# Graph attention on one core: edge projection and Q's selection produced with edges on partitions

## The chip, the cores and the metric

The kernel runs on one core of a Trainium2 chip. The metric is device time in microseconds (us) of one execution, lower is better. Engines: PE is TensorE, DVE is VectorE, ACT is ScalarE, POOL is GpSimd, SP is SyncE, which issues most plain transfers. "A gather" below is one indirect DMA that GpSimd issues: it fetches one row per partition for 128 edges.

## The reference, cut to what matters

One graph-attention layer with 8 heads of 16 columns over 12,500 nodes and 212,500 edges sorted by destination, then a residual, a batch norm over the nodes, a second residual and a layer norm.

```python
Q, K, V = x @ WQ, x @ WK, x @ WV              # 12500 x 128, as 8 heads of 16
Eh = edge_attr_128 @ WE                       # 212500 x 128
score = K[src] * Q[dst] / sqrt(16) * Eh       # per edge, 128 columns
score = exp(clip(score.sum(-1), -5, 5))       # per edge and head
wV = segment_sum(V[src] * score, dst);  Z = segment_sum(score, dst)
h = x + wV / (Z + 1e-6)
h = batchnorm(h) * gamma + beta
out = layernorm(x + h)
```

## The kernel before

**Layout.** Edges are cut into 1661 tiles of 128. A group `g` has two halves of four tiles (`halves(g)`; `G = 8`, `U = 4`), there are 208 groups, and the last one has 3 + 2 tiles. The destinations of one half lie in a window of 64 nodes.

**Set-up.** A table of K and V (`kvd`, one row of 256 floats per node) is computed from x and written to DRAM (`table_rows`, L634). Meanwhile GpSimd gathers rows of x for the first 64 tiles, eight groups; these are turned (`turn_x`, L261) and projected (`project`, L268), three groups during set-up and the other five ("late" groups) inside the loop.

**Gathers.** Every later tile needs one gather of K and V, 128 rows of 1 KB (L202), issued in order on GpSimd's own queue. `load_kv` queues the eight gathers of a group as soon as a slot is free; after the start there are nine slots, so the gathers of group g + 9 wait for `message(g)`.

**The loop** (L759 to L822) is written out by hand: each engine runs its instructions in the order of these calls, and nothing reorders them. Iteration g works on several groups at once. What each step does, with its line:

- `eh_mm` (L510), for g + 2: the edge projection, as two matmuls with `WE` stationary and the transposed edge features moving, so that the result has columns on partitions and 512 edges along the row. `eh_out` (L517): ScalarE copies it to SBUF (`wt`).
- `q_mm`, `q_out` (L483, L487), for g + 4: Q of the group's two windows, to SBUF as float32. `q_hi`, `q_rest`, `q_mid`, `q_lo` (L491 to L501), for g + 3 and g + 2: Q is split into three bfloat16 parts, two steps on ScalarE and two subtractions on VectorE.
- `turned_onehot` (L473), for g + 3: a bfloat16 one-hot matrix (node against edge). `qe_mm` (L525), for g + 2: six matmuls, three parts by two halves, select Q for each edge.
- `both` (L535), for g + 1: VectorE multiplies the two in columns-on-partitions form. `turn_back` (L543), for g + 1: eight transposes on TensorE bring the product to edges on partitions.
- `products` (L558), for g: VectorE multiplies the gathered K in place by it, one instruction for each half. This is the first step that needs the gather.
- `scores` (L565), `clip_exp` (L574 to L576), `message` (L580), for g: the score by head, its exponential, and V times it.
- `onehot` (L463 to L466) and `gather_sum` (L595, L596): the sum over edges into nodes on TensorE, for g - 1.
- `denom`, `recip`, `attn` (L605, L608, L612), for g - 2, and `add_x`, `x_out` (L621, L622, L626), for g - 3: the quotient and the residual.

**PSUM.** Eight banks: two named `ps_e`, two `ps_q`, two `ps_t`, one `ps_a` and one `ps_m`.

**The end** (L823 to L889, then `last_stage`): the last two groups half by half, the norm's sums, and the layer norm over all nodes.

Of the kernel before, what the change touches and what calls it, by code (L numbers as in the profile page):

```python
# [8 lines left out]
F32 = mybir.dt.float32  # L9
BF16 = mybir.dt.bfloat16  # L10
# [7 lines left out]
P = 128  # L18
# [42 lines left out]
def gnn_kernel(  # L61
# [199 lines left out]
    def turn_x(g, a, act=None):  # L261
        XT[g, a] = wp.tile([P, 4, P], F32, name="xt", bufs=2)
        ps = turned()
# [4 lines left out]
    def project(g, a, ps_kv, act=None):  # L268
        for c in (0, 2):
            ps = ps_kv()  # L270
# [151 lines left out]
    EA, OH, OT, Q3, XW, BASE, MSG, QE, OS, AT, AGG, WT, PW = ({} for _ in range(13))  # L422
# [13 lines left out]
    def project_main(g):  # L436
        half = [table_tile(2 * (g % 2) + a) for a in (0, 1)]
        KV[g] = lambda a, b, c, n=P: half[a // 4][:, a % 4:a % 4 + b - a, c:c + n]
        for a in (0, 4):
            project(g, a, lambda: turned().rearrange("p (a b) d -> p a (b d)", b=2), True)  # L440
# [28 lines left out]
    def turned_onehot(g):  # L469

        OT[g] = wp.tile([P, U * P], BF16, name="ot", bufs=2)
        if usizes[2 * g] == usizes[2 * g + 1] == U:
            nc.vector.tensor_scalar(OT[g], RB[g], wiota, None, op0=OP.is_equal)  # L473
# [5 lines left out]
    PQ, QS, QR = {}, {}, {}  # L479
# [9 lines left out]
    def q_hi(g):  # L489
        Q3[g] = wp.tile([P, 3, P], BF16, name="q3", bufs=2)  # L490
        nc.scalar.activation(Q3[g][:, 0, :], QS[g], AF.Copy)  # L491

    def q_rest(g):
        QR[g] = QS[g]
        nc.vector.tensor_sub(QR[g], QS[g], Q3[g][:, 0, :])

    def q_mid(g):
        nc.scalar.activation(Q3[g][:, 1, :], QR[g], AF.Copy)

    def q_lo(g):  # L500
        nc.vector.tensor_sub(Q3[g][:, 2, :], QR[g], Q3[g][:, 1, :])  # L501

    EH = {}

    def eh_mm(g):

        EH[g] = []
        for a, b in halves(g):
            eh = psp.tile([P, U * P], F32, name="ps_e", bufs=2)[:, :(b - a) * P]
            nc.tensor.matmul(eh, w_e, EA[g][:, a:b, :].rearrange("p a b -> p (a b)"), start=True, stop=True)  # L510
            EH[g].append(eh)

    def eh_out(g):
        WT[g] = []
        for h, (a, b) in enumerate(halves(g)):
            t = wp.tile([P, U * P], F32, name="wt", bufs=4)
            nc.scalar.activation(t[:, :(b - a) * P], EH[g][h], AF.Copy)  # L517
            WT[g].append(t)

    def qe_mm(g):  # L520
        QE[g] = [psp.tile([P, U * P], F32, name="ps_q", bufs=2)[:, :(b - a) * P] for a, b in halves(g)]
        for k in range(3):
            for h, (a, b) in enumerate(halves(g)):
                r = slice(h * WN, (h + 1) * WN)
                nc.tensor.matmul(QE[g][h], Q3[g][r, k, :], OT[g][r, :(b - a) * P], start=(k == 0), stop=(k == 2))  # L525

    def ehqe(g):
        eh_mm(g)
        eh_out(g)
        qe_mm(g)  # L530

    def both(g, h):
        a, b = halves(g)[h]
        t = WT[g][h][:, :(b - a) * P]
        nc.vector.tensor_tensor(t, t, QE[g][h], op=OP.mult)  # L535

    def turn_back(g):

        PW[g] = []
        for h, (a, b) in enumerate(halves(g)):  # L540
            ps = turned()
            for j in range(b - a):
                nc.tensor.transpose(ps[:, j, :], WT[g][h][:, j * P:(j + 1) * P], ident)  # L543
            PW[g].append(ps)
# [9 lines left out]
    def products(g, hs=(0, 1)):  # L554
        for i in hs:
            a, b = halves(g)[i]
            kv = KV[g](a, b, 0)
            step = nc.vector.tensor_tensor(kv, kv, PW[g][i][:, :b - a, :], op=OP.mult)  # L558
            PARTS.setdefault(g, []).append(step)
# [58 lines left out]
    def add_x(g):  # L618
        NEW[g] = ps = (psp.tile([P, 4, P], F32, name="ps_t", bufs=2)[:, 0, :] if NG - 3 <= g < NG - 1 else
                       small_ps[:, 1, :] if g >= NG - 4 else sum_ps[:, W + P:W + 2 * P])  # L620
# [40 lines left out]
    def both_halves(g):  # L661
        both(g, 0)
        both(g, 1)


    steps = [[(locate,)], [(place, runs[0])], [], [(q_mm, 0), (q_out, 0), (q_hi, 0)],
             [(q_rest, 0), (q_mid, 0), (load_rel, 0)], [(q_lo, 0), (load, 0)],
             [(q_mm, 1), (q_out, 1), (q_hi, 1), (load_rel, 1)],
             [(q_rest, 1), (q_mid, 1)], [(q_lo, 1), (load_rel, 2)], [(load, 1)], [(turned_onehot, 0)],
# [4 lines left out]
    for q in range(NQ):  # L674
# [11 lines left out]
        for g, a in piece.get(q, []):  # L686
            project(g, a, wide)
# [9 lines left out]
    ehqe(0)  # L697
    q_mm(2)
    q_out(2)
    q_hi(2)  # L700
    both_halves(0)
    q_rest(2)
    q_mid(2)
    turn_back(0)
    ehqe(1)
    within(load, 2)
    turned_onehot(2)
    load_rel(3)
    q_window(3)
    q_window(4)  # L710
    q_mm(3)
    q_out(3)
    load_rel(4)
    load(3)
# [17 lines left out]
    RING = ["ps_e", "ps_e", "ps_q", "ps_q", "ps_t", "ps_t", "ps_a", "ps_m"]  # L732
# [26 lines left out]
    for g in range(NG - 2):  # L759
        within(load, g + 4)  # L760
        within(load_rel, g + 5)
        if (g + 6) % RQ == 0 and (g + 6) // RQ in quads:
            load_quad((g + 6) // RQ)
        within(q_hi, g + 3)
        within(products, g)
        within(q_lo, g + 2)
# [4 lines left out]
        within(turned_onehot, g + 3)  # L771
        within(both_halves, g + 1)
# [29 lines left out]
        within(q_mid, g + 3)  # L802
# [29 lines left out]
    both_halves(last)  # L832
    attn(g - 2)
    add_x(g - 3)
    issue()
    gather_sum(g - 1)
# [3 lines left out]
    turn_back(last)  # L840
# [309 lines left out]
```

## Time and profile before

| | |
|---|---|
| median of 3 runs | 2141.98 us (2141.85 to 2142.24) |
| the profiled execution, its own time | 2143.53 us |
| its span, first to last instruction | 2141.1 us |
| mean granted TensorE clock | 0.917 |
| PE busy | 1710.7 us (80%) |
| DVE busy | 1590.1 us (74%) |
| ACT busy | 670.6 us (31%) |
| POOL busy | 1606.6 us (75%) |
| mean DMA rate | 180 GB/s |

Busy time is the union of an engine's instructions. A row of a group of instructions reads: line, engine, operation, output <- inputs, shape, count | busy us, mean ns of one | idle time of the engine just before them, and what ended most of it. "<-issue" means that no wait that the profile knows ended just then. A row of a timeline reads: start us, duration us, engine, line, operation, and in brackets the idle time before it.

### The profile page before, as it was taken

The page shows a single profiled execution, that of the slowest core. Times are in us where ns is not written, and L with a number is a line of the kernel's source. Part 1 is how long each engine was busy: PE and PEld are TensorE (multiplying, and loading weights), DVE is VectorE, ACT ScalarE, POOL GpSimd, SP SyncE. Part 2 cuts the span into 40 slices and gives each one's busy share as a digit, 9 for nine tenths or more (in the row PEclk, how much of TensorE's full clock was granted, in tenths as well). Part 3 has the DMA queues.
Part 4 walks back from the last instruction along what each step waited for, and adds up shares of the span by engine and source line. Part 5 has one row for each costly group of instructions (what it writes and reads, how often), then busy time and mean ns, then how long its engine had stood idle before and what let it go on. Part 6 is the DMA issues. An engine that isn't in the chain of part 4 may idle for free. (4 is left out here: it accounts for less than half of the span.)

```text
span 2141.1 us, 31269 instructions
## 1 busy us (share of the span) xinstructions
PE 1710.7 (80%) x9414; PEld 1100.9 (51%) x9414; DVE 1590.1 (74%) x3555; ACT 670.6 (31%) x2688; POOL 1606.6 (75%) x1697
## 2 busy tenths in 40 slices
PE   8899998777868778877778778777878877778777
PEld 7576565444545445544445445545545545544456
DVE  4679998777777777777677777677777777777786
ACT  3454343223223223222223223223223222223225
POOL 7777777777777777777777777777777777777775
PEclk9999999998998998899898998898898898898899
DMA  9957666565565565565565565565565565565574
GB/s 306 308 177 201 188 198 183 165 182 166 165 183 158 171 183 163 167 183 165 165 183 158 172 183 163 167 184 160 169 184 159 170 184 161 167 184 164 170 235 125
DMA packets 172648, 386.41 MB, mean 180 GB/s; under 512 B 35950, under 2 KB 88727, under 8 KB 172471
## 3 DMA queue, kind: packets, MB, share of 16 engines
q0 software_dynamic: 78704, 213.62, 34.6%
q1 hardware_dynamic: 90404, 169.36, 25.9%
q8 instruction: 78, 1.28, 0.3%
q10 hardware_dynamic: 3363, 1.34, 0.2%
q14 instruction: 99, 0.81, 0.1%
HBM read 364.56 MB, written 19.63 MB: 179 GB/s over the span
## 5 line engine op out<-in xcount | busy, mean ns | idle before, releaser
L202 POOL DMA_INDIRECT slot<-kvd,srcs x1597 | 1517.8, 950 | 486.4 <-issue 409.4
L558 DVE TENSOR_TENSOR slot<-slot,ps_t 128x512 f32<-128x512 f32 x410 | 276.7, 682 | 453.2 <-DMA slot<-kvd,srcs 412.3
L543 PE MATMUL ps_t<-ident,wt 128*128 128x128 f32 x1661 | 283.9, 313 | 385.9 <-DVE wt L535 384.1
L596 PE MATMUL ps_a<-msg,oh 128*128 128x136 f32 (+1 forms) x3322 | 524.4, 297 | 2.1 <-DVE msg L580 2.1
L543 PEld LDWEIGHTS ps_t<-ident,wt 128*128 128x128 f32 x1661 | 211.7, 159 | 562.3 <-issue 501.2
L596 PEld LDWEIGHTS ps_a<-msg,oh 128*128 128x128 f32 (+1 forms) x3322 | 425.2, 171 | 81.5 <-issue 53.8
L575 ACT ACTIVATE ps_m<-s 128x64 f32<-128x64 f32 (+1 forms) x209 | 47.5, 227 | 1125.4 <-DVE s L574 1060.9
L510 PE MATMUL ps_e<-ea,w_e 128*128 128x512 f32 x832 | 390.6, 591 | 0.7 <-ACT wt L517 0.7
L535 DVE TENSOR_TENSOR wt<-wt,ps_q 128x512 f32<-128x512 f32 x416 | 264.4, 675 | 2.6 <-PE ps_q L525 2.6
L580 DVE TENSOR_TENSOR msg<-slot,ps_m 128x1024 f32<-128x1024 f32 (+2 forms) x209 | 248.0, 1188 | 0.4 <-ACT ps_m L575 0.3
L565 DVE TENSOR_REDUCE s<-slot 128x64 f32<-128x1024 f32 (+1 forms) x208 | 248.1, 1194 | 0.1
L517 ACT ACTIVATE wt<-ps_e 128x512 f32<-128x512 f32 x416 | 233.8, 620 | 13.3 <-PE ps_e L510 13.2
L525 PE MATMUL ps_q<-ot,q 64*128 64x512 bf16 x1248 | 213.3, 457 | 0.0
L510 PEld LDWEIGHTS ps_e<-ea,w_e 128*128 128x128 f32 x832 | 143.0, 190 | 100.7 <-issue 98.5
L463 DVE TENSOR_TENSOR oh<-ps_m,rel_i 128x512 f32<-128x512 f32 x208 | 141.4, 680 | 0.0
L491 ACT ACTIVATE q<-qs 128x128 bf16<-128x128 f32 x208 | 64.3, 309 | 217.3 <-PE ps_q L525 186.6
L621 PEld LDWEIGHTS ps_a<-ident,at 128*128 128x128 f32 x408 | 71.7, 221 | 111.7 <-issue 56.0
L621 PE MATMUL ps_a<-ident,at 128*128 128x128 f32 x408 | 115.4, 370 | 2.5 <-DVE relrow L322 2.3
L626 ACT ACTIVATE hx<-ps_a 128x64 f32 x408 | 87.9, 215 | 33.9 <-PE ps_a L596 27.2
L452 ACT ACTIVATE xw<-hx 128x64 f32 x416 | 88.2, 280 | 11.1 <-DMA hx<-xT 6.5
L525 PEld LDWEIGHTS <-q 64*128 64x128 bf16 x1248 | 48.9, 103 | 80.9 <-issue 64.4
L622 PE MATMUL ps_a<-xw,ident 128*128 128x128 f32 x408 | 89.7, 306 | 0.0
(175 smaller groups left out, 1618.9 us busy)
## 6 DMA issues: line engine op xcount, KB each, us to landing
ea<-eaT SPq DMA_DIRECT2D x207, 512.0 KB, 3.8
slot<-kvd,srcs POOLq DMA_INDIRECT x1597
rbq<-relT SPq DMA_DIRECT2D x94, 256.0 KB, 6.6
kvd<-slot SPq DMA_DIRECT2D x12, 512.0 KB, 7.1
kvd<-t SPq DMA_DIRECT2D x12, 512.0 KB, 6.8
slot<-xT SPq DMA_DIRECT2D x24, 256.0 KB, 5.2
out<-o SPq DMA_DIRECT2D x23, 256.0 KB, 3.2
hx<-xT SPq DMA_DIRECT2D x11, 512.0 KB, 7.7
```

The lines of the kernel that those rows point to most:

```text
L202: return nc.gpsimd.indirect_dma_start(out=out, out_offset=None, in_=table, in_offset=bass.IndirectOffsetOnAxis(ap=srcs[:, e:e + 1], axis=0))
L463: nc.vector.tensor_tensor(one, iota_ps[:, None, :].to_broadcast([P, n, P]), r[:, :n, None].to_broadcast([P, n, P]), op=OP.is_equal)
L510: nc.tensor.matmul(eh, w_e, EA[g][:, a:b, :].rearrange("p a b -> p (a b)"), start=True, stop=True)
L517: nc.scalar.activation(t[:, :(b - a) * P], EH[g][h], AF.Copy)
L525: nc.tensor.matmul(QE[g][h], Q3[g][r, k, :], OT[g][r, :(b - a) * P], start=(k == 0), stop=(k == 2))
L535: nc.vector.tensor_tensor(t, t, QE[g][h], op=OP.mult)
L543: nc.tensor.transpose(ps[:, j, :], WT[g][h][:, j * P:(j + 1) * P], ident)
L558: step = nc.vector.tensor_tensor(kv, kv, PW[g][i][:, :b - a, :], op=OP.mult)
L565: step = nc.vector.tensor_reduce(SS[g][:, a:b, :], KV[g](a, b, 0).rearrange("p t (h d) -> p t h d", d=DH), axis=AX.X, op=OP.add)
L580: step = nc.vector.tensor_tensor(MSG[g][:, a:b, :P].rearrange("p t (h d) -> p t h d", d=DH), KV[g](a, b, P).rearrange("p t (h d) -> p t h ...
L596: nc.tensor.matmul(AGG[g][WN if j >= n else 0:], OH[g][j], MSG[g][:, j, :], start=(j == 0), stop=(j == n - 1))
L621: nc.tensor.matmul(ps, AT[g], ident, start=True, stop=False)
```

## The change

- The edge projection has the edge features stationary and `WE` moving, one matmul for each tile, so that its result lies in PSUM with edges on partitions.
- Q's selection is one float32 matmul for each tile: the one-hot matrix (now float32) stationary, the half's float32 Q moving. The three-part split is gone.
- `products` multiplies the gathered K twice, by the one and by the other, both read from PSUM. `eh_out`, `both` and `turn_back` are gone.
- One ring of six PSUM banks (`ps`) takes the place of `ps_e`, `ps_q` and `ps_t`. A group's four results fill four of the six, so its first half is computed before `gather_sum` and its second half after it, for g + 1 in iteration g.
- The steps ahead run at smaller distances: `load` g + 3, `load_rel` g + 4, `turned_onehot` g + 2, `q_mm` and `q_out` g + 2, `q_window` g + 3.
- `add_x` of the last four groups writes to `ps_m`.

```diff
+    def bank():
+        return psp.tile([P, 4, P], F32, name="ps", bufs=6)
+
     def wide():
-        t = psp.tile([P, 4, P], F32, name=("ps_e", "ps_q")[turn[0] % 2], bufs=2)
-        return t.rearrange("p (a b) d -> p a (b d)", b=2)
-
-    def turned():
-        return psp.tile([P, 4, P], F32, name="ps_t", bufs=2)
+        return bank().rearrange("p (a b) d -> p a (b d)", b=2)
...
     def turned_onehot(g):
-        OT[g] = wp.tile([P, U * P], BF16, name="ot", bufs=2)
+        OT[g] = wp.tile([P, U * P], F32, name="ot", bufs=2)
...
-    def q_hi(g):
-    def q_rest(g):
-    def q_mid(g):
-    def q_lo(g):
-    def eh_mm(g):
-    def eh_out(g):
-    def qe_mm(g):
-    def both(g, h):
-    def turn_back(g):
+    def eh_qe(g, hs=(0, 1)):
+        for h in hs:
+            a, b = halves(g)[h]
+            r = slice(h * WN, (h + 1) * WN)
+            EH[g, h], QE[g, h] = bank(), bank()
+            for j in range(a, b):
+                nc.tensor.matmul(EH[g, h][:, j - a, :], EA[g][:, j, :], w_e, start=True, stop=True)
             for j in range(b - a):
+                nc.tensor.matmul(QE[g, h][:, j, :], OT[g][r, j * P:(j + 1) * P], QS[g][r], start=True, stop=True)
...
             kv = KV[g](a, b, 0)
-            step = nc.vector.tensor_tensor(kv, kv, PW[g][i][:, :b - a, :], op=OP.mult)
+            nc.vector.tensor_tensor(kv, kv, EH[g, i][:, :b - a, :], op=OP.mult)
+            step = nc.vector.tensor_tensor(kv, kv, QE[g, i][:, :b - a, :], op=OP.mult)
...
     for g in range(NG - 2):
-        within(load, g + 4)
-        within(load_rel, g + 5)
+        within(load, g + 3)
+        within(load_rel, g + 4)
-        within(q_hi, g + 3)
         within(products, g)
-        within(q_lo, g + 2)
         within(denom, g - 2)
         within(scores, g)
         within(clip_exp, g)
         within(recip, g - 2)
-        within(turned_onehot, g + 3)
-        within(both_halves, g + 1)
+        within(turned_onehot, g + 2)
...
         within(add_x, g - 3)
-        within(q_mm, g + 4)
+        within(q_mm, g + 2)
...
+        if not late_x:
+            eh_qe(g + 1, (0,))
         within(gather_sum, g - 1)
-        if not late_x:
-            within(eh_mm, g + 2)
         within(x_out, g - 3)
-        within(q_out, g + 4)
+        within(q_out, g + 2)
         within(sums_out, g - 1)
         if late_x:
             project_main(g + 1)
-            within(eh_mm, g + 2)
-        within(eh_out, g + 2)
-        within(q_window, g + 5)
-        within(turn_back, g + 1)
-        within(qe_mm, g + 2)
+            eh_qe(g + 1, (0,))
+        eh_qe(g + 1, (1,))
+        within(q_window, g + 3)
         within(attn, g - 2)
-        within(q_rest, g + 3)
-        within(q_mid, g + 3)
         within(message, g)
         within(onehot, g + 1)
...
     products(g, (0,))
-    both_halves(last)
     attn(g - 2)
     add_x(g - 3)
     issue()
+    eh_qe(last, (0,))
     gather_sum(g - 1)
     x_out(g - 3)
     sums_out(g - 1)
     products(g, (1,))
-    turn_back(last)
+    eh_qe(last, (1,))
```

More of the change, by code (lines that the diff above doesn't have):

```diff
@@ L420, in load_x @@
                 nc.sync.dma_start(XR[i][:, :width(i)], xT[:, i * B4:i * B4 + width(i)])
-    EA, OH, OT, Q3, XW, BASE, MSG, QE, OS, AT, AGG, WT, PW = ({} for _ in range(13))
+    EA, OH, OT, XW, BASE, MSG, QE, OS, AT, AGG = ({} for _ in range(10))
     def nt(g):
@@ L487, in q_out @@
         nc.scalar.activation(QS[g], PQ[g], AF.Copy, scale=0.25)
-    def q_hi(g):
-        Q3[g] = wp.tile([P, 3, P], BF16, name="q3", bufs=2)
-        nc.scalar.activation(Q3[g][:, 0, :], QS[g], AF.Copy)
-    def q_rest(g):
-        QR[g] = QS[g]
-        nc.vector.tensor_sub(QR[g], QS[g], Q3[g][:, 0, :])
-    def q_mid(g):
-        nc.scalar.activation(Q3[g][:, 1, :], QR[g], AF.Copy)
-    def q_lo(g):
-        nc.vector.tensor_sub(Q3[g][:, 2, :], QR[g], Q3[g][:, 1, :])
-    EH = {}
-    def eh_mm(g):
[L507 to L511, printed above, removed]
-    def eh_out(g):
[L514 to L518, printed above, removed]
-    def qe_mm(g):
[L521 to L530, printed above, removed]
-    def both(g, h):
-        a, b = halves(g)[h]
-        t = WT[g][h][:, :(b - a) * P]
-        nc.vector.tensor_tensor(t, t, QE[g][h], op=OP.mult)
-    def turn_back(g):
-        PW[g] = []
-        for h, (a, b) in enumerate(halves(g)):
-            ps = turned()
+    EH = {}
+    def eh_qe(g, hs=(0, 1)):
[5 more added lines that the diff above has]
+                nc.tensor.matmul(EH[g, h][:, j - a, :], EA[g][:, j, :], w_e, start=True, stop=True)
             for j in range(b - a):
-                nc.tensor.transpose(ps[:, j, :], WT[g][h][:, j * P:(j + 1) * P], ident)
-            PW[g].append(ps)
+                nc.tensor.matmul(QE[g, h][:, j, :], OT[g][r, j * P:(j + 1) * P], QS[g][r], start=True, stop=True)
     SENT, PARTS = {}, {}
@@ L618, in add_x @@
     def add_x(g):
-        NEW[g] = ps = (psp.tile([P, 4, P], F32, name="ps_t", bufs=2)[:, 0, :] if NG - 3 <= g < NG - 1 else
-                       small_ps[:, 1, :] if g >= NG - 4 else sum_ps[:, W + P:W + 2 * P])
+        NEW[g] = ps = small_ps[:, g % 2, :] if g >= NG - 4 else sum_ps[:, W + P:W + 2 * P]
         nc.tensor.matmul(ps, AT[g], ident, start=True, stop=False)
@@ L660, in gnn_kernel @@
         piece.setdefault(3 + k * (NQ - 4) // (2 * early), []).append((k // 2, 4 * (k % 2)))
[L661 to L669, printed above, removed]
+    steps = [[(locate,)], [(place, runs[0])], [], [(q_mm, 0), (q_out, 0)],
+             [(load_rel, 0)], [(load, 0)],
+             [(q_mm, 1), (q_out, 1), (load_rel, 1)],
+             [], [(load_rel, 2)], [(load, 1)], [(turned_onehot, 0)],
              [(turned_onehot, 1)]]
@@ L696, in gnn_kernel @@
     load_kv()
[L697 to L705, printed above, removed]
+    eh_qe(0)
     within(load, 2)
-    turned_onehot(2)
     load_rel(3)
[L709 to L714, printed above, removed]
     onehot(0)
@@ L731, in gnn_kernel @@
     AHEAD = [0, 1, 2, 3, 4, 5, 6, 12, 18]
-    RING = ["ps_e", "ps_e", "ps_q", "ps_q", "ps_t", "ps_t", "ps_a", "ps_m"]
+    RING = ["ps"] * 6 + ["ps_a", "ps_m"]
     def blocks(i):
```

12 lines of the change are left out of this document (6 added, 6 removed).

## The prediction

> **What bounds the kernel now.** I began with the busy times and then asked for GpSimd's own rows, because a busy share of three quarters hides what fills the rest.
>
> ```profile
> PE 1710.7 (80%) x9414; PEld 1100.9 (51%) x9414; DVE 1590.1 (74%) x3555; ACT 670.6 (31%) x2688; POOL 1606.6 (75%) x1697
> ```
>
> No engine looks full. The costliest group of instructions and the view of its line (shortest, median and longest duration) say more:
>
> ```profile
> L202 POOL DMA_INDIRECT slot<-kvd,srcs x1597 | 1517.8, 950 | 486.4 <-issue 409.4
> ```
>
> ```profile
> L202 POOL DMA_INDIRECT slot<-kvd,srcs x1597: 942/946/1197, 83.4 to 2086.4; - x200
> ```
>
> A gather takes 0.946 us, and 486.4 / 1597 = 0.304 us lies ahead of each: a pitch of 1.25 us. GpSimd's timeline, first and last of 1661 gathers:
>
> ```profile
> 3.04 1.15 POOL L202 DMA_INDIRECT slot<-x,srcs  x1 [1.87 <-DMA srcs<-src]
> ...
> 2086.38 0.95 POOL L202 DMA_INDIRECT slot<-kvd,srcs  x1 [0.30 <-issue]
> ```
>
> From 3.04 to 2087.33 are 2084.3 us, and 1661 x 1.25 = 2076. So there is no wait longer than the 0.30 us gap anywhere: the gathers are one unbroken line, and 53.8 us follow it. The execution's own 2143.53 us are 3.0 of start + 2084.3 + 53.8 + 2.4 outside the span. The time can change in only three ways: gathers wait, a gather itself takes another time, or the last 53.8 us change. Eight gathers, 10.0 us, are the budget of a group.
>
> The gathers do not all take 0.946. The mean is 0.950, so 1517.8 - 1597 x 0.946 = 7.0 us are excess. I set the start of each gather against what VectorE was running. In 54 cases a gather of over 0.995 us begins while `attn` (L612) or `q_rest` (L495) runs, 5.3 us in all; the first and the last:
>
> ```profile
> 99.63 0.28 DVE L495 TENSOR_TENSOR qs<-qs,q 128x128 f32<-128x128 f32 x1
> 99.65 1.08 POOL L202 DMA_INDIRECT slot<-kvd,srcs  x1 [0.30 <-issue]
> ...
> 2031.24 0.28 DVE L495 TENSOR_TENSOR qs<-qs,q 128x128 f32<-128x128 f32 x1
> ...
> 2031.30 1.03 POOL L202 DMA_INDIRECT slot<-kvd,srcs  x1 [0.30 <-DVE wt L535]
> ```
>
> The first gather is 0.13 too long and L495 ends 0.26 after its start; the second 0.087, and 0.22. Both fit one rule: a gather needs something 0.13 us after its start that the VectorE instruction holds until its own end, if that instruction started at least 0.02 us sooner. The holders read two SBUF tensors, or are the one-hot (L473). Products with PSUM (L558, L535) hold nobody up.
>
> [...]
>
> **Where VectorE stands against the gathers.** One period of VectorE from the moment T at which the last gathered rows of a group land, and GpSimd in the same stretch:
>
> ```profile
> 1009.69 0.69 DVE L558 TENSOR_TENSOR slot<-slot,ps_t 128x512 f32<-128x512 f32 x1 [1.92 <-DMA slot<-kvd,srcs]
> 1010.29 0.28 DVE L501 TENSOR_TENSOR q<-qs,q 128x128 bf16<-128x128 f32 x1
> 1010.49 0.17 DVE L605 TENSOR_SCALAR rz<-os 128x8 f32<-128x8 f32 x1
> 1010.57 1.21 DVE L565 TENSOR_REDUCE s<-slot 128x64 f32<-128x1024 f32 x1
> 1011.81 0.23 DVE L574 TENSOR_SCALAR s<-s 128x64 f32<-128x64 f32 x1
> 1011.96 0.19 DVE L608 RECIPROCAL rz<-rz 128x8 f32<-128x8 f32 x1
> 1012.08 0.30 DVE L473 TENSOR_SCALAR ot<-rbq,wiota 128x512 bf16<-128x512 bf16 x1
> 1012.29 1.27 DVE L535 TENSOR_TENSOR wt<-wt,ps_q 128x512 f32<-128x512 f32 x2
> 1013.49 0.34 DVE L612 SCALAR_TENSOR_TENSOR at<-os,keep,rz 128x128 f32<-128x128 f32 x1
> 1013.75 0.28 DVE L495 TENSOR_TENSOR qs<-qs,q 128x128 f32<-128x128 f32 x1
> 1013.95 1.21 DVE L580 TENSOR_TENSOR msg<-slot,ps_m 128x1024 f32<-128x1024 f32 x1
> ```
>
> ```profile
> 1006.82 0.95 POOL L202 DMA_INDIRECT slot<-kvd,srcs  x1 [0.30 <-issue]
> ...
> 1013.07 0.95 POOL L202 DMA_INDIRECT slot<-kvd,srcs  x1 [0.30 <-DVE wt L535]
> ```
>
> T = 1009.69 is 2.87 us after the start of the group's last gather, 1006.82, so VectorE's steps stand at a fixed phase to the gathers: five pitches later a gather starts at T + 3.38. Now the one-hot runs at T + 2.39 to 2.69 and `attn` with `q_rest` at T + 3.80 to 4.34, so that gather starts in the free stretch between. In 88 of the 165 groups from 40 to 204 this distance is 2.82 to 2.94 us; in the others other transfers make it longer, at any phase.
>
> **The change part by part.**
>
> *TensorE.* Busy times of what goes, and the loads of fourteen float32 pairs (weight load and matmul) in a dense stretch:
>
> ```profile
> L510 PE MATMUL ps_e<-ea,w_e 128*128 128x512 f32 x828 | 389.3, 592 | 0.7 <-ACT wt L517 0.7
> ...
> L543 PE MATMUL ps_t<-ident,wt 128*128 128x128 f32 x1661 | 283.9, 313 | 385.9 <-DVE wt L535 384.1 <-DVE slot L558 1.0
> ...
> L525 PE MATMUL ps_q<-ot,q 64*128 64x512 bf16 x1242 | 212.6, 458 | 0.0
> ```
>
> ```profile
> 1015.68 1.78 PEld L596 LDWEIGHTS ps_a<-msg,oh 128*128 128x128 f32 x14
> ```
>
> (389.3 + 283.9 + 212.6) / 208 = 4.26 us of a group go. A float32 matmul is two pairs here (L543, a transpose, is one for each tile, L510 two for each half), so 8 tiles x 2 matmuls x 2 = 32 pairs come, at 1.78 / 14 = 0.127: 4.07 us. TensorE stays at 1710.7 / 208 - 0.2 = 8.0 us of the 10.0. The order adds a wait: the second half of g + 1 takes the banks of the first half of g, so it stands behind that product, and `add_x`, `q_mm` and the next first half are queued behind it. VectorE makes that product when four gathers have landed, about 5 us ahead of T, so the wait has ended long before T. Cost nothing, under cover of the 2 us that TensorE has over.
>
> *ScalarE.* Three copies of the group go. It is 31% busy; nothing on the line of gathers waits for it. Nothing.
>
> *VectorE, total.* `q_rest` and `q_lo` go (0.28 each). `both` becomes the second multiply of `products`: the same count, shape and operand kinds. The one-hot writes float32. The nearest row of a float32 VectorE comparison:
>
> ```profile
> L311 DVE TENSOR_SCALAR lim<-lim 128x416 f32<-128x416 f32 x1 | 0.4, 421 | 0.0
> ```
>
> For 512 elements that is between 0.42 and 0.42 x 512 / 416 = 0.52; against it stand 0.30 (L473, if only the input's type counts) and 0.69 (L558's full rate). I take 0.47, nearest to L311. In all 1590.1 / 208 = 7.6 us become 7.6 - 0.56 + 0.17 = 7.2 of 10.0: still under the budget, so nothing directly.
>
> [...]
>
> *VectorE, phase.* This is what I take to count. After T two multiplies depend on each other. A dependent neighbour starts 0.04 us after the end:
>
> ```profile
> 2090.70 0.42 DVE L558 TENSOR_TENSOR slot<-slot,ps_t 128x256 f32<-128x256 f32 x1 [1.22 <-DMA slot<-kvd,srcs]
> 2091.16 0.42 DVE L565 TENSOR_REDUCE s<-slot 128x16 f32<-128x256 f32 x1
> ```
>
> So the second starts at T + 0.72, `scores` at T + 1.44 (now 0.88), and the one-hot, 1.50 later as now, at T + 2.94 to 3.41. `attn` follows directly, since `both` no longer stands between: like L535 after L473 it starts 0.09 before the end, so T + 3.32 to 3.66. The gather that starts at T + 3.38 needs the port at 3.51 and gets it at 3.66: 0.15 us late. It happens where the gather starts 0.02 or more after `attn`, a distance of at most 2.91 us: 66 of 165 groups, 83 of 208, so 83 x 0.15 = 12.5 us. [...] The 5.3 us at `attn` and `q_rest` go, since `q_rest` is the instruction that holds in nearly all of them. The groups at other phases pay for 0.72 us of one-hot and `attn` where they pay for 0.92 of three instructions now; I count that as even. Net +7.
>
> Bounds: with VectorE 0.15 us earlier or later by a little more, `attn` misses all of them: 0 - 5.3 = -5. If the one-hot catches them instead, 111 x 0.25 (twice L473's hold) = 28, net +22.
>
> *The last 53.8 us.* The last product (2090.70) waited for its rows, and VectorE had 1.22 us to spare. The second multiplies of group 206's second half (0.72) and of group 207's first (0.57) take those, and the last one adds 0.42 + 0.04: +0.5.
>
> *The start.* `eh_mm` ran two groups ahead, now one. The five late groups are TensorE's:
>
> ```profile
> 105.60:160.00 54.40, 54.40 (x334) 39.53 (x333) 39.07 (x96) 30.09 (x89) 41.06 (x44) 1.00 0.58 176
> ```
>
> Its busy time fills the stretch, 11 us a group. The tightest point after it is the slot of group 8, given free by `message(8)` and refilled by group 17:
>
> ```profile
> 162.03 1.21 DVE L580 TENSOR_TENSOR msg<-slot,ps_m 128x1024 f32<-128x1024 f32 x1
> ```
>
> ```profile
> 173.92 0.94 POOL L202 DMA_INDIRECT slot<-kvd,srcs  x1 [0.30 <-issue]
> ```
>
> 10.7 us to spare. With TensorE's work equal, nothing; the cover ends at 10.7 / 5 = 2.1 us more for each late group. The SP loads keep their distance from use (`load` and its reader both moved by one), so no queue is newly blocked.
>
> **The sum.** 2143.53 + 7 + 0.5 = 2151.0 for a profiled execution. The median of the runs lies 1.55 below the profiled one now, so the forecast is 2149.
>
> **The rivals.** About 0.2% (4.3 us) is what a measurement of this kernel can tell from no change.
>
> *Clear of the port* (18%). `q_rest`'s holds go and `attn` falls between gathers. It decides within 0.1 us of phase, and the multiply's true delay or a one-hot of 0.30 would do it. 2142 - 5.3 + 0.5 = 2137.
>
> *The one-hot catches the gathers* (15%). It needs 0.1 to 0.2 us more delay than I reckon. Net +13 to +22, so 2155 to 2165.
>
> *TensorE becomes the bound* (3%). If a pair cost 0.30, the mean of one matmul, and not 0.127, a group would take 8.2 - 4.26 + 32 x 0.30 = 13.5 us: some 700 us slower. It decides from 0.19 a pair. Dense rows speak against it.
>
> *The start stalls* (4%). With 4 us more for each late group, 20 - 10.7 = 9 us: 2158.
>
> *The change does little because all of it is hidden*, the two phase terms cancelling: this is the lower part of my forecast case, +0.5 to +4.
>
> **The numbers.** My case (60%) reaches from 2142.5 to 2155, a third of it within 0.2%. Faster by over 0.2% comes from the first rival alone: 0.14. Within: 0.20 from my case, 0.04 and 0.02 from the first rival and the start: 0.26. Slower: 0.60. The range from 2137 to 2165 leaves out TensorE, part of the one-hot's case and little else.
>
> **What would show it.** Right: gathers still without a wait over 0.3 us; the gathers' mean above 0.950 with the median at 0.946, the long ones starting just after `attn`; the one-hot at about 0.47; the stretch after the last gather 54.3. Wrong: a gather released late by a VectorE or TensorE instruction; a mean at or below 0.947; VectorE no longer waiting for the rows.

## The result, and the profile after

| | before | after |
|---|---|---|
| median | 2142.62 us (20 runs, 2141.57 to 2145.00) | 2146.86 us (20 runs, 2144.05 to 2152.67) |
| the profiled execution, its own time | 2143.53 us | 2144.05 us |
| its span | 2141.1 us | 2142.3 us |
| granted TensorE clock | 0.917 | 0.903 |

After to before is 1.0020, 95% interval 1.0013 to 1.0027: slower by 0.2%. The profiled execution of the changed kernel is the fastest of its 20, 2.8 us under their median, so its trace shows only a part of the loss. Three of the six groups of experiments ran in a disturbed state, told under 4, in which every kernel, that of before included, took some 600 us or more longer: their times are not set beside this table, and only the lengths of their gathers are used.

The page after, first the busy times, then the gathers (group, and the view of the line), then GpSimd's first and last gather in its timeline:

```profile
PE 1866.8 (87%) x12317; PEld 1605.0 (75%) x12317; DVE 1577.8 (74%) x3139; ACT 362.9 (17%) x1856; POOL 1607.0 (75%) x1697
...
L202 POOL DMA_INDIRECT slot<-kvd,srcs x1597 | 1518.1, 951 | 486.5 <-issue 410.9
```

```profile
L202 POOL DMA_INDIRECT slot<-kvd,srcs x1597: 942/946/1212, 83.6 to 2086.9; - x200
```

```profile
3.08 1.15 POOL L202 DMA_INDIRECT slot<-x,srcs  x1 [1.92 <-DMA srcs<-src]
...
2086.92 0.95 POOL L202 DMA_INDIRECT slot<-kvd,srcs  x1 [0.30 <-DVE rz L563]
```

The gathers are still one line without a wait over 0.32 us. They are busy 1518.1 us, 0.3 more than before, the last ends at 2087.87 in place of 2087.33, and 54.4 us follow where 53.8 did. That is the whole of the +1.2 us between the two profiled spans: +0.5 at the gathers and +0.7 at the end.

The median is equal and the sum is longer, so again a few gathers are long. Setting each gather against VectorE's rows: 33 are held by the one-hot (L472; 3.6 us), 36 by `attn` (L567; 3.3 us), and 9 by the one-hot in a way I had not seen before (0.9 us). One of the first kind, in VectorE's timeline and GpSimd's:

```profile
1044.50 0.43 DVE L472 TENSOR_SCALAR ot<-rbq,wiota 128x512 f32<-128x512 bf16 x1
1044.85 0.34 DVE L567 SCALAR_TENSOR_TENSOR at<-os,keep,rz 128x128 f32<-128x128 f32 x1
```

```profile
1044.62 1.12 POOL L202 DMA_INDIRECT slot<-kvd,srcs  x1 [0.30 <-issue]
1046.05 0.95 POOL L202 DMA_INDIRECT slot<-kvd,srcs  x1 [0.30 <-issue]
```

The gather starts 0.12 us into the one-hot and is 0.18 us too long: 0.13 + 0.18 after its start the one-hot ends, the rule of the prediction.

And one of the new kind:

```profile
261.39 0.44 DVE L472 TENSOR_SCALAR ot<-rbq,wiota 128x512 f32<-128x512 bf16 x1
```

```profile
260.88 1.07 POOL L202 DMA_INDIRECT slot<-kvd,srcs  x1 [0.30 <-issue]
```

Here the one-hot starts 0.51 us after the gather, and the gather ends at 261.95, 0.12 after the one-hot's end at 261.83. So a gather can be kept waiting a second time, about 0.82 us after its start. "The port" in the prediction and the expectations is a name for whatever it waits for at these two moments; the traces show the moments, which I call its first and second need, and not what lies behind them. (The score step, L520, lies across the first moment in such places too, but it is not the holder: in run 3 it lies there 186 times and no gather is long.)

### The profile page after: what moved, and what is told of

Read it like the earlier page. It is cut to its first block, busy times and chain, and to the rows that moved or that the text cites. A ratio compares the mean times of both kernels' runs of the same rounds, so it can differ in the third digit from the quotient of the medians.

```text
span 2142.3 us, 36046 instructions
## 1 busy us (share of the span) xinstructions
PE 1866.8 (87%) x12317; PEld 1605.0 (75%) x12317; DVE 1577.8 (74%) x3139; ACT 362.9 (17%) x1856; POOL 1607.0 (75%) x1697
## 5 line engine op out<-in xcount | busy, mean ns | idle before, releaser
L202 POOL DMA_INDIRECT slot<-kvd,srcs x1597 | 1518.1, 951 | 486.5 <-issue 410.9
L551 PE MATMUL ps_a<-msg,oh 128*128 128x136 f32 (+1 forms) x3322 | 579.7, 317 | 1.0 <-DVE msg L535 1.0
L512 DVE TENSOR_TENSOR slot<-slot,ps 128x512 f32<-128x512 f32 x410 | 279.3, 681 | 404.2 <-DMA slot<-kvd,srcs 332.2
L498 PE MATMUL ps<-qs,ot 64*128 64x128 f32 x3322 | 517.8, 300 | 0.0
L496 PE MATMUL ps<-w_e,ea 128*128 128x128 f32 x3322 | 486.5, 295 | 0.0
L498 PEld LDWEIGHTS ps<-qs,ot 64*128 64x128 f32 x3322 | 434.8, 201 | 56.0 <-issue 12.6
L496 PEld LDWEIGHTS ps<-w_e,ea 128*128 128x128 f32 x3322 | 451.6, 210 | 1.2
L513 DVE TENSOR_TENSOR slot<-slot,ps 128x512 f32<-128x512 f32 x410 | 281.4, 686 | 29.7 <-PE ps L498 1.3
L520 DVE TENSOR_REDUCE s<-slot 128x64 f32<-128x1024 f32 (+1 forms) x208 | 249.9, 1202 | 0.2
L482 PE MATMUL ps_a<-w_q,xw 128*128 128x128 f32 x416 | 92.5, 309 | 0.0
L465 DVE TENSOR_TENSOR oh<-ps_m,rel_i 128x256 f32<-128x256 f32 x208 | 86.8, 417 | 0.0
L472 DVE TENSOR_SCALAR ot<-rbq,wiota 128x512 f32<-128x512 bf16 x188 | 84.7, 450 | 0.3
L550 PE MATMUL ps_a<-os,carry 64*1 64x136 f32 x414 | 83.7, 283 | 0.0
```

The source lines that it names most:

```text
L202: return nc.gpsimd.indirect_dma_start(out=out, out_offset=None, in_=table, in_offset=bass.IndirectOffsetOnAxis(ap=srcs[:, e:e + 1], axis=0))
L482: return nc.tensor.matmul(PQ[g], XW[g], w_q, start=True, stop=True)
L496: nc.tensor.matmul(EH[g, h][:, j - a, :], EA[g][:, j, :], w_e, start=True, stop=True)
L498: nc.tensor.matmul(QE[g, h][:, j, :], OT[g][r, j * P:(j + 1) * P], QS[g][r], start=True, stop=True)
L512: nc.vector.tensor_tensor(kv, kv, EH[g, i][:, :b - a, :], op=OP.mult)
L513: step = nc.vector.tensor_tensor(kv, kv, QE[g, i][:, :b - a, :], op=OP.mult)
```

## The experiments

Two theories stand in the expectations. *Port theory*: the loss is gathers made longer by VectorE. *TensorE theory* (first called *clock theory*): TensorE, 87% busy, is late in the changed kernel, and its granted clock sets the time.

Runs 1 to 3 are of the table's kind; those under 4 are the disturbed ones.

**1. The holders moved between the gathers.**

```diff
-        within(products, g)
         within(denom, g - 2)
-        within(scores, g)
-        within(clip_exp, g)
         within(recip, g - 2)
+        within(products, g)
         within(turned_onehot, g + 2)
+        within(attn, g - 2)
+        within(scores, g)
+        within(clip_exp, g)
...
-        within(attn, g - 2)
         within(message, g)
```

`at` has two buffers in it.

> The same kernel as clear_2: one-hot and attn between products and scores. Port theory: wherever VectorE's and TensorE's results are seen at once and the gathers stand without a wait over 0.32 us, the sum of gather lengths over 0.945 is below 6 us and the time 2141 to 2144, no slower than the kernel before. TensorE theory: 2145 to 2149 as the changed kernel. Where the gathers wait for hundreds of us again, the time is some 2900 and only the lengths can be read: below 5 us over 0.945.

2152.56 us (5 runs) against 2144.81 for the kernel before, ratio 1.0035 (1.0021 to 1.0049). The gathers, the last of them, and the two holders:

```profile
L202 POOL DMA_INDIRECT slot<-kvd,srcs x1597 | 1524.3, 955 | 486.7 <-issue 407.4
```

```profile
2093.28 0.95 POOL L202 DMA_INDIRECT slot<-kvd,srcs  x1 [0.30 <-issue]
```

```profile
L472 DVE TENSOR_SCALAR ot<-rbq,wiota 128x512 f32<-128x512 bf16 x188 | 100.4, 534 | 0.0
...
L567 DVE SCALAR_TENSOR_TENSOR at<-os,keep,rz 128x128 f32<-128x128 f32 x208 | 71.1, 342 | 0.2
```

My number failed, and the theory stands better for it. I had put the pair between two first needs. At T + 1.4 the one-hot meets the second need of the gather that started at T + 0.9 (18 gathers of this kind, 1.6 us), it is itself stretched, from 0.45 to 0.53 us in the mean, so `attn` comes up to 0.2 us later than I had it and holds 80 gathers (6.1 us). The gathers are busy 6.2 us more than in the changed kernel, and their last ends 6.4 us later, with no gap over 0.32 us. Holds make 4.0 of the 6.2; the rest is 1 to 2 ns on each gather, whose cause is not shown. TensorE did the same work at the same clock (0.903) and would have left the time as it was. The other 3.2 us stand after the last gather; I take them to be `attn` and its inputs, which now come late there, but no run separates that.

**2. Neither holder as it was.** The one-hot reads and writes with a stride of 128 elements; `attn` goes to ScalarE.

```diff
-            nc.vector.tensor_scalar(OT[g], RB[g], wiota, None, op0=OP.is_equal)
+            nc.vector.tensor_scalar(OT[g].rearrange("p (t j) -> p j t", j=P), RB[g].rearrange("p (t j) -> p j t", j=P),
+                                    wiota, None, op0=OP.is_equal)
...
-        nc.vector.scalar_tensor_tensor(
...
+        rk = wp.tile([P, H], F32, name="rk", bufs=2)
+        nc.scalar.activation(rk, RZ[g], AF.Copy, scale=keep[:, g:g + 1])
+        for h in range(H):
+            nc.scalar.activation(AT[g][:, h * DH:(h + 1) * DH], OS[g][:, h * DH:(h + 1) * DH], AF.Copy,
+                                 scale=rk[:, h:h + 1])
```

> The changed kernel without either holder: the one-hot reads and writes with a stride of 128 elements (one element at a time, some 0.69 us in place of 0.44), attn is made by ScalarE (one factor a head, nine instructions of some 0.2 us). Nothing is left out. Port theory, with the time as 2080 + 54.4 + the sum of gather lengths over 0.945 + 0.3 (that sum fits the profiled executions of before, after and clear_3 to within 1 us): the sum falls from 9.4 to about 2 us, no gather over 0.995 us begins under the one-hot or attn, 2136 to 2139 us and less spread between executions than the 8.6 us of the changed kernel. TensorE theory (the loss of 4 us is TensorE's, late by its lower clock): unchanged, 2145 to 2149. Where the gathers wait for hundreds of us, only the lengths can be read: below 3 us over 0.945.

2171.37 us (4 runs), ratio 1.0142 (1.0120 to 1.0164): 28 us slower than before, 22.0 of them in the gathers' row and 5.7 after the last gather.

```profile
L202 POOL DMA_INDIRECT slot<-kvd,srcs x1597 | 1539.8, 964 | 486.5 <-issue 401.2
```

```profile
2108.66 0.95 POOL L202 DMA_INDIRECT slot<-kvd,srcs  x1 [0.30 <-DVE s L530]
```

```profile
L472 DVE TENSOR_SCALAR ot<-rbq,wiota 128x512 f32<-128x512 bf16 x188 | 135.4, 720 | 0.0
```

I expected a one-hot with a stride to hold nobody, which no run had shown. It takes 0.72 us, where the plain one takes 0.45 in the mean, and holds at both points: of 111 gathers whose first need fell under it 85 were long (20.0 us), of 79 at the second need 41 (9.6 us). `attn` on ScalarE held none. So a slow one-hot holds as a fast one does. What is left is that its operands all lie in SBUF, and that it is longer. The next run separates these two.

**3. The one-hot as long, with one operand in PSUM.**

```diff
+    wiota_ps = small_ps[:, 1, P - 1:]
+    nc.vector.tensor_copy(wiota_ps, wiota)
...
-            nc.vector.tensor_scalar(OT[g], RB[g], wiota, None, op0=OP.is_equal)
+            nc.vector.tensor_tensor(OT[g], RB[g], wiota_ps.to_broadcast([P, U * P]), op=OP.is_equal)
...
         within(scores, g)
+        within(turned_onehot, g + 2)
         within(clip_exp, g)
         within(recip, g - 2)
-        within(turned_onehot, g + 2)
```

It stands ahead of `clip_exp` because the bank is the one that ScalarE's exponential writes, and behind it the one-hot would wait for that.

> The changed kernel with one thing taken from the one-hot: its column of numbers lies in PSUM, so it is a tensor_tensor with one SBUF and one PSUM operand, as the products are, some 0.69 us in place of 0.44; it stands between scores and clip_exp. Nothing is left out; attn stays as it is. Port theory, sharpened by the runs so far (a gather needs the port 0.13 us and again 0.82 us after its start; the end of the last gather is 2078.4 us plus the sum of lengths over 0.945 in before, after, clear_3 and no_port to within 0.2 us): no gather is held by the one-hot, also not at its second point; the sum falls from 9.4 to 3 to 6 us, the last gather ends at 2081.5 to 2084.5, the time is 2137.5 to 2141. Length theory (no_port lost because its one-hot is longer, whatever its operands): a sum of 20 us or more, 2155 or more. TensorE theory: 2145 to 2149 as the changed kernel. Where the gathers wait for hundreds of us, only the lengths can be read: none long under the one-hot.

2140.27 us (11 runs, 2137.90 to 2143.75) against 2142.93 for the kernel before (15 runs), ratio 0.9988 (0.9979 to 0.9997): faster than both kernels.

```profile
L204 POOL DMA_INDIRECT slot<-kvd,srcs x1597 | 1512.5, 947 | 486.5 <-issue 405.8
...
L474 DVE TENSOR_TENSOR ot<-rbq,ps_m 128x512 f32<-128x512 bf16 x188 | 127.4, 678 | 0.0
```

```profile
2081.26 0.95 POOL L204 DMA_INDIRECT slot<-kvd,srcs  x1 [0.30 <-issue]
```

The one-hot is 0.68 us, nearly as long as in the run before. 69 gathers had their first need under it and 129 their second: the longest of them all is 0.949 us. `attn`, left as it was, holds 26 (1.9 us). The instruction's form changed too, but that is not the cure: `q_rest` in the kernel before is a `tensor_tensor` with both operands in SBUF, and it held. One place, with the one-hot running from 0.40 before the gather's start to 0.28 after it:

```profile
110.64 0.68 DVE L474 TENSOR_TENSOR ot<-rb,ps_m 128x512 f32<-128x512 bf16 x1
```

```profile
111.04 0.95 POOL L204 DMA_INDIRECT slot<-kvd,srcs  x1 [0.30 <-issue]
```

The length theory is gone. Over the five profiled executions of this kind, the end of the last gather less the busy time in the gathers' row is one constant:

| | gathers busy | last one ends | difference | span after it |
|---|---|---|---|---|
| before | 1517.8 | 2087.33 | 569.5 | 53.8 |
| after | 1518.1 | 2087.87 | 569.8 | 54.4 |
| run 1 | 1524.3 | 2094.23 | 569.9 | 57.6 |
| run 2 | 1539.8 | 2109.61 | 569.8 | 59.5 |
| run 3 | 1512.5 | 2082.21 | 569.7 | 55.3 |

TensorE's busy time went from 1711 to 1867 us among them, and this difference does not show it.

**4. The disturbed runs.** How they differ: where ScalarE copies the first turned rows of x to SBUF, in ScalarE's and TensorE's timelines of the kernel before.

```profile
17.09 0.60 ACT L249 ACTIVATE xt<-ps_t 128x512 f32<-128x512 f32 x1 [3.17 <-remote]
```

```profile
13.03 0.60 PE L265 MATMUL ps_t<-ident,slot 128*128 128x128 f32 x4
```

The transposes end at 13.63 and ScalarE starts on them at 17.09, with no row in between that it waits for. In the undisturbed profile the same step starts at 13.55, the transposes having ended at 13.19. From there on the gathers wait for slots. Nor is it only that results are seen late: TensorE's own matmuls come late, with no wait ended that the profile knows. Two rows of the view of waits (total us, times, longest), of the kernel before and of the changed one in this state:

```profile
PE ps_t L543 <- issue: 138.3, 125, 4.0
```

```profile
PE ps L496 <- issue: 246.6, 317, 2.0
```

Over all lines TensorE's gaps of this kind (over 0.15 us) come to 385 us in the kernel before and 583 in the changed one; in the five profiles of run 3's table there is none. What brings the state about is not shown.

*The changed kernel and the kernel before, again.*

> The changed kernel once more, for a second trace. Port theory (gathers are held at their start by VectorE's one-hot and attn, and nothing else moves the time): the sum of the gathers' lengths over 0.945 us, 9.4 us in the first trace with an own time of 2144.05, accounts for the own time of this execution too, to within 1 us: own time = 2144.05 + (sum - 9.4). Rival (clock theory: TensorE at 87% and a granted clock of 0.90 sets the run's time): the own time follows the clock, the sum of the long gathers stays at 9 to 10 us, and some gathers start late, with gaps over 0.31 us ahead of them. Median 2146 to 2148 by either.

> The kernel before, for its own profile on the chip of this call. The table shows 2768 us for it on a chip that granted TensorE 0.81. Port theory (gathers lengthened by VectorE explain the difference of the two kernels): wherever the granted clock is 0.90 or more, one unbroken line of gathers again, sum of the lengths over 0.945 at 9 us, time 2142; at a clock near 0.8 it says nothing. TensorE theory (TensorE's work for a group divided by the granted clock is set against the 10 us of eight gathers): at 0.9 the same, at 0.8 a time above 2700 us with GpSimd idle for over 1000 us behind TensorE's results, TensorE in the same slices at full share.

> The changed kernel again, for a second profiled execution. Port theory: own time is 2133 us plus the sum of the gather lengths over 0.945, to within 1 us (2144.05 with 9.4 in the first), and no gather stands longer than 0.32 us behind the one ahead. TensorE theory: in an execution slower than the first, gathers stand longer than 0.32 us behind the one ahead, released late by VectorE steps that in turn waited for TensorE; their sum is the difference to 2144.05. At a granted clock below 0.8 the time is some 2940 us.

> The changed kernel once more: the profiled execution in the table took 2144.05, the median of 20 is 2146.86, and what the other 2.8 us are is not in that one trace. Port theory: the last gather ends at 2078.4 us plus the sum of gather lengths over 0.945, to within 0.3; the stretch after it is 54.4; own time is the sum of the two and 1.8. So an execution of 2147 has a sum of some 12 us and one of 2150 some 15, and the excess over 9.4 stands in gathers held by the one-hot or attn, in groups of other phases. TensorE theory: the sum stays at 9 to 10 and what is over 2144 stands as gaps of more than 0.32 us between gathers, or after the last one.

The changed kernel took 2938.67, 2903.41 and 2903.17 us against 2768.33, 2742.68 and 2741.81 for the kernel before: 1.0608 (1.0578 to 1.0638), 1.0589 (1.0556 to 1.0622) and 1.0592 (1.0567 to 1.0617). The kernel before, run once for its own profile, took 2748.66 us; its gathers waited 555 us beyond their usual gaps, and TensorE was busy in 70% of the span, not at the full share that the TensorE theory had. The granted clock was 0.77 to 0.79 against 0.81. The question that the last of these was to answer, where the 2.8 us between the profiled execution and the median stand, stays without a trace.

*The holders moved, as in run 1.*

> VectorE's one-hot and attn are moved between products and scores (T + 1.4 to 2.1), where no gather starts in the usual phase; nothing else is changed but a second buffer for attn's result and denom and recip ahead of products. Port theory: long gathers sum to 1 to 4 us and not 9.4, the median falls from 2146.9 to 2136 to 2141, below both kernels. Clock theory: within 2 us of the changed kernel, 2145 to 2149, as TensorE's work is the same.

> One-hot and attn put between products and scores, at T + 1.4 to 2.1, between the gathers that start at T + 0.88 and T + 2.13. Nothing is left out. Port theory: sum of lengths over 0.945 down from 9.4 to about 6 us, 2143 to 2144 us on a chip at 0.90 or more. TensorE theory: unchanged against the changed kernel, within 2 us; below 0.8 a little slower than it, since scores and message come 0.7 us later after the gathers have landed.

2957.78 us (1.0684, 1.0649 to 1.0718) and 2936.16 us (1.0697, 1.0661 to 1.0732). In the second, the gathers held by the pair are long by 0.6 us in sum against 3.7 in the changed kernel beside it: gathers that wait for slots start at other phases, and here the pair misses them, as it did not in run 1.

*VectorE later by 0.3 us* (two copies of 128 and 16 elements from PSUM ahead of the one-hot):

> Two copies from PSUM (128 and 16 elements, about 0.3 us together, no port) are put ahead of the one-hot, so that it ends at T + 3.7 and the gathers that start at T + 3.3 to 3.4 fall inside it. Port theory: each such group pays 0.15 to 0.25 us, long gathers sum to 17 to 30 us, median 2153 to 2166. Clock theory: VectorE has slack, so 2146 to 2149.

2941.87 us (1.0625, 1.0596 to 1.0654), no different from the changed kernel beside it. But `attn` now holds 129 gathers for 9.6 us, all by 0.06 to 0.08 us, where it held 17 for 1.5 there. One of them:

```profile
258.83 0.52 DVE L472 TENSOR_SCALAR ot<-rb,wiota 128x512 f32<-128x512 bf16 x1
259.27 0.33 DVE L567 SCALAR_TENSOR_TENSOR at<-os,keep,rz 128x128 f32<-128x128 f32 x1
```

```profile
258.16 0.95 POOL L202 DMA_INDIRECT slot<-kvd,srcs  x1 [0.30 <-issue]
259.41 1.02 POOL L202 DMA_INDIRECT slot<-kvd,srcs  x1 [0.30 <-issue]
```

The one-hot starts 0.67 us into a gather and takes 0.52 us where it takes 0.48 with nothing in its way. In this run 129 one-hots that start 0.54 to 0.68 us into a gather are stretched, to between 0.52 and 0.66 us, and all of them end 1.19 to 1.20 us after the gather's start. So `attn`, which follows, always starts 0.14 us ahead of the next gather. The two lock, which is why the holds come in runs of equal size.

*The one-hot and the reciprocal both through PSUM*, in the order of the changed kernel (in run 3 the one-hot with its column in PSUM takes 0.68 us in the mean, in the changed kernel 0.45, so VectorE has 0.23 us a group more to do):

> [...] Port theory: long gathers sum to 1 to 3 us, median 2136 to 2140, although VectorE has 0.25 us a group more to do. Clock theory, or any theory in which VectorE's length counts: 2146 to 2200.

3716.08 us (1.3431, 1.3402 to 1.3461). The reciprocal had gone into the bank of TensorE's sums, so `attn` waited for them, 1853.5 us in all: the time tells nothing of the holds. The lengths do: 30 gathers under the one-hot at the first need and 158 at the second, none long.

*One-hot and Q in bfloat16:*

> The changed kernel with one-hot and Q in bfloat16, Q in one part (its lower parts are left out), so eight bf16 matmuls take the place of eight float32 ones of two pairs, some 1.3 us or more of TensorE a group less, and the one-hot takes 0.30 again in place of 0.44. Port theory: at a clock of 0.90 or more the sum of lengths over 0.945 falls by 1 us at most and the time with it, 2145 to 2147. TensorE theory: the loss goes, 2142 to 2143, with a distance of at most 2.94 us between a group's last gather and its product in 80 or more of the 165 groups (59 with the change, 88 before); below 0.8 the time falls from 2940 to 2770 or lower.

2945.93 us (1.0745, 1.0710 to 1.0781), 42 us slower than the changed kernel beside it although TensorE was busy 1874.8 us in place of 2164.9; its clock was 0.72. So even there TensorE's busy time is not what sets the time, and the TensorE theory, at 2770 or lower, missed by 176 us. What makes the changed kernel 6% slower in these runs is open. A lead is TensorE's gaps without a known wait: 385 us in the kernel before, 583 in the changed one, 706 in this run, the order of their times. That they are the cause was not tested.

## Why the prediction was right, step by step

**The bound** was read rightly: one unbroken line of gathers, whose lengths and the stretch after them are the time. The table of run 3 is that reading in five kernels.

**VectorE's phase** came out as worked out. `scores` starts 1.51 us after T (reckoned 1.44: `denom` slips in ahead of it), the one-hot 2.99 (2.94), `attn` 3.34 (3.32). The one-hot takes 0.433 in the median, 0.450 in the mean, where I took 0.47.

**The +7 for the held gathers** is the term that was mis-sized. The profiled execution shows +0.3 to +0.5. What the port of this term is, no run shows; what the runs show are gathers of 0.946 us in the median that take up to 1.197 us in the kernel before and 1.212 in the changed one, where `attn`, the one-hot or `q_rest` runs at a need. The term was added up from two parts, and both were wrong, in opposite directions.

The first part was `attn` in the groups at the usual phase: 83 gathers by 0.15 us, 12.5 in all. Fewer groups stand there, 59 of 165, where 88 did. In 87 of the other 106 the product waited for rows that landed later, in 5 for TensorE; why the rows land later is not shown. (The row is of all products; by far the most of their idle time ends with rows.)

```profile
L512 DVE TENSOR_TENSOR slot<-slot,ps 128x512 f32<-128x512 f32 x410 | 279.3, 681 | 404.2 <-DMA slot<-kvd,srcs 332.2 <-PE ps_a L551 42.9 <-PE ps L498 13.2
```

But the step that failed is another. In 58 of these 59 groups `attn` ran at the gather's first need, as I had it, and it held only 5 gathers, 0.6 us in all. I had let it hold where it starts 0.02 us sooner than the gather, which I had read off `q_rest`. In this trace `attn` held a gather only where it started at least 0.07 us sooner. In 28 of the groups it started 0.02 to 0.06 us sooner; there the gather went first, and `attn` was stretched instead, by up to 0.05 us. One place of each kind, the first not held and the second held:

```profile
460.72 0.38 DVE L567 SCALAR_TENSOR_TENSOR at<-os,keep,rz 128x128 f32<-128x128 f32 x1
...
771.61 0.34 DVE L567 SCALAR_TENSOR_TENSOR at<-os,keep,rz 128x128 f32<-128x128 f32 x1
```

```profile
460.77 0.94 POOL L202 DMA_INDIRECT slot<-kvd,srcs  x1 [0.30 <-DVE rz L563]
...
771.68 1.09 POOL L202 DMA_INDIRECT slot<-kvd,srcs  x1 [0.30 <-DVE rz L563]
```

The second part was the 5.3 us at `attn` and `q_rest` that were to go, with the groups at other phases "even". In the kernel before, all but 0.1 of the 6.7 us of holds in the loop (5.3 `attn` and `q_rest`, 1.0 the one-hot, 0.4 `q_lo`) stood in groups at other phases, so these could not both lose 5.3 us and stay even. What came of them: `q_rest`'s 4.4 us went, but the one-hot's holds rose from 1.0 us to 4.4, of which 0.9 at the second need, and `attn`'s from 0.9 to 3.3, of which 2.6 at other phases. Of `attn`'s 36 holds 23 are by 0.07 us, the locked kind shown under 4. In all 6.7 us of holds became 7.7, and not 14.

**The median** of 2149 was therefore met within 2 us in part by luck. The profiled execution was to take 2151.0 and took 2144.05. I had carried over that the median lies 1.55 below the profiled execution, and it lies 2.8 above. By the table of run 3 an execution of 2146.9 would have its gathers busy 3 us longer. That is inferred, not shown. What run 3 shows is that without the one-hot's holds the profiled execution falls by 4.7 us (5.6 less in the gathers' row, 0.9 more at the end) and the median by 6.6.

**The end**: +0.7 for the +0.5 I had. VectorE no longer waits for the last rows (the product is the page's L558 before, L512 now):

```profile
2091.50 0.41 DVE L512 TENSOR_TENSOR slot<-slot,ps 128x256 f32<-128x256 f32 x1
2091.95 0.42 DVE L513 TENSOR_TENSOR slot<-slot,ps 128x256 f32<-128x256 f32 x1
```

**TensorE**, which I put at 8.0 us a group, takes 1866.8 / 208 = 9.0.

```profile
L498 PE MATMUL ps<-qs,ot 64*128 64x128 f32 x3322 | 517.8, 300 | 0.0
L496 PE MATMUL ps<-w_e,ea 128*128 128x128 f32 x3322 | 486.5, 295 | 0.0
```

(517.8 + 486.5) / 6644 = 0.151 us a pair, not 0.127. My price came from a dense stretch at full clock (granted 1.00 from 1015.68 to 1017.46 in the kernel before). In such a stretch of the changed kernel (1.00 from 1015.96 to 1018.02) the loads of eight pairs still take 0.96 to 0.98 us:

```profile
1015.96 0.98 PEld L496 LDWEIGHTS ps<-w_e,ea 128*128 128x128 f32 x8
1017.06 0.96 PEld L498 LDWEIGHTS ps<-qs,ot 64*128 64x128 f32 x8
```

Two things are left out of that price. At full clock the matmuls' rows come to 0.139 us a pair, since each burst ends with the 0.27 us of its last matmul; and 779 of the 6644 pairs ran at half clock (granted 0.50), at 0.252. The effect that the trace shows is late groups of 11.8 us (T of group 3 at 102.1, of group 7 at 149.3) in place of 11.0 ("with TensorE's work equal, nothing" was 4 us short, of the 10.7 of cover that I had named). No gather waited for it.

**VectorE in total** stayed at 7.6 us a group where I had 7.2. The two subtractions that went overlapped the rows on each side of them by 0.08 us, so they freed 0.12 of their 0.28 each; the second multiply, which starts 0.035 us after the first has ended, adds 0.64 us to the busy time, where an instruction of `both` added 0.56; and the one-hot came to 0.12 more.

**The rivals.** "Clear of the port" is what happened in the groups at the usual phase, where `attn` held nobody in 54 of 59. Its price did not come, because the holds at other phases stayed. Run 3, which frees only the one-hot, gains 2.7 us on the kernel before, against the 5 of that rival, with 1.9 us at `attn` and 1.6 at the end still paid. "The one-hot catches the gathers" (its 111 gathers were the 88 of 165 groups, taken for 208) is run 2, with 22 us in the gathers' row, and a part of it, 4.4 us, is in the changed kernel. The start did not stall.

## What to carry to other kernels

Where one engine's unbroken line of work is the bound, look at the lengths of its instructions and not only at its gaps: holds of 0.05 to 0.4 us on 26 to some 140 of 1661 gathers set runs 1 to 3 up to 27 us apart. A margin read off one holder is not that of another: `q_rest`'s 0.02 us put on `attn` was the largest error here. Moving the instruction that holds them is a gamble on phase, which in run 1 the feedback between the two engines settled against me; taking away what it holds with (here one operand moved to PSUM, though it made VectorE's instruction half as long again) was the one edit that paid. And a price read in a dense stretch of TensorE is a price at full clock and without the ends of bursts: 0.127 us a pair there, 0.151 in the whole.

## What the runs showed of the hardware that I had not expected

*A gather can be kept waiting at two moments*, 0.13 and about 0.82 us after its start, and they are not alike. At the first, every holder keeps it to its own end (the strided one-hot to about 0.1 us before its end), if it started soon enough, and how soon differs: in the kernel before `q_rest` held all 42 gathers that it met there having started first, the last of them 0.005 us ahead; in the changed kernel `attn` held from 0.07 us ahead and not at 0.064, the one-hot at 0.038 and not at 0.033.

*At the second moment only the one-hot counts, and who started first decides.* In the changed kernel the 12 one-hots that started up to 0.53 us after a gather and ran past 0.83 all held it. The 26 that started 0.53 to 0.76 us after it were themselves stretched, to 0.47 to 0.67 us, and held nobody; they ended 1.19 us after the gather's start, or up to 1.23. Those that started later were not stretched. So the gather keeps the one-hot out for a part of its own length alone. `q_rest`, with two SBUF inputs, lay across this moment 121 times in the kernel before: no gather was over 0.949 us, and it was never over 0.289 us itself.

*What sets the one-hot apart from `q_rest` is not shown.* `q_rest` reads two tensors in SBUF; the one-hot reads one, and a column with one number a partition. At the first moment both hold. At the second run 2's strided one-hot (0.72 us) held 41 of 79 gathers, as the plain one does and `q_rest` does not. Whether that lies in its column or in its operation, no run separates. With the column in PSUM, and the operation changed with it (run 3), no gather was over 0.949 us, of 69 at the first moment and 129 at the second.

*TensorE's granted clock falls to 0.50 for 3.41, 6.83 or 10.24 us.* Four windows of 2 us in the changed kernel (the columns are the stretch, busy time of PE, PEld, DVE, ACT and POOL, granted clock, DMA):

```profile
1004.00:1006.00 2.00, 0.00 (x0) 0.00 (x0) 1.97 (x6) 0.89 (x6) 1.39 (x3) 0.89 0.33 105
1006.00:1008.00 2.00, 1.76 (x8) 1.76 (x9) 1.97 (x4) 0.48 (x4) 1.64 (x2) 0.50 0.43 129
...
1014.00:1016.00 2.00, 2.00 (x10) 1.19 (x9) 0.70 (x1) 0.00 (x0) 1.39 (x3) 0.55 0.29 94
1016.00:1018.00 2.00, 2.00 (x18) 1.88 (x17) 1.69 (x4) 1.17 (x6) 1.64 (x2) 1.00 0.44 129
```

After 3.9 us without a matmul the granted clock falls to 0.50 at 1005.55 and comes back at 1015.79, 10.24 us later and 9.5 us after the matmuls began again. In the clock's record all but one of each kernel's half-clock stretches are 3.41, 6.83 or 10.24 us long; the changed kernel has 63 of them, 419 us in all and 6.83 in the median, the kernel before 77, 359 us and 3.41. The two longer lengths are twice and three times 3.41; 38 of the changed kernel's 63 stretches are longer than 3.41. Why a stretch begins, and what sets its length, the traces do not show.
